# Cross-attention on one core: VectorE's sums interleaved, four products regrouped in PSUM, and the order of GpSimd's sums changed

## The chip, the cores and the metric

The kernel runs on one core of a Trainium2 chip. The metric is the device time of one execution in microseconds (us), and the median of the runs is compared. Engines are called as the profile calls them: PE (TensorE's matmuls), PEld (its weight loads), DVE (VectorE), ACT (ScalarE), POOL (GpSimd) and SP (SyncE, which here only issues DMAs). "Lnnn" is a line of the kernel file.

## The reference, cut to what matters

```python
q = jnp.einsum('bcn,dc->bnd', x1, Wq) + bq
k = jnp.einsum('bcn,dc->bdn', x2, Wk) + bk[:, None]
v = jnp.einsum('bcn,dc->bdn', x2, Wv) + bv[:, None]
attn = jax.nn.softmax(jnp.einsum('bnd,bdm->bnm', q, k), axis=2)
attn_out = jnp.einsum('bcm,bnm->bcn', v, attn)
return attn_out + x1
```

There are 8 batches; x1 and x2 have 512 channels and 1024 positions each, q and k have 64 channels. Everything is float32.

## The kernel before, in words

**The algebra.** The kernel never forms v. With e = exp(scores - maximum), transposed, it computes y = x2 · e (512 x 512 x 1024 after the halves are put side by side), scales y by one over the column sums of e, and then computes result = Wv · y + bv + x1. Both big products are done by a Strassen-Winograd scheme: the left and the right factor are cut into 2 x 2 quarters ("11", "12", "21", "22"), four sums of left quarters (S1 to S4) and four of right quarters (T1 to T4) are formed, and seven products take the place of eight. The table `MULT` says which left and right block each product takes and in which PSUM bank pair (a or c) it is accumulated. The products of y run in the order 1, 2, 6, 5, 7, 3, 4, those of the result in the order 1, 6, 2, 5, 7, 3, 4. One batch is one pass of `period`. I number batches from 0, as the code does (`s.b`); the batch after s is called n, the one after that nn.

**Plain and in blocks.** A plain product of y is 8 matmuls of 128 x 512 columns (`multiply`, L365); a plain product of the result is 4. The trace records each float32 matmul as two instructions, so a row with "x16" is a plain product of y and one with "x8" is a plain product of the result. A product "in blocks" is split by the same seven-product scheme once more: `inner_left` (L412, four DVE operations) and `inner_right` (L421, three) form its inner sums, and seven inner products (`inner_product`, L438) of two matmuls of 128 x 256 take the place of eight quarters: 14 matmuls of 128 x 256, each row "x4" being one inner product. Two ways exist to collect the inner products:

- `multiply_seeded` (L459): the chain of products 1, 6, 5 is accumulated in one buffer of the pool `ps_s`, product 7 in the other; ACT copies the chain at the right moments into two fresh banks of the pool `ps_a` (L479), where the other inner products are accumulated on it, and `complete` lets DVE add the copy of product 7, v, onto the second bank (L485). In y this is used for products 1, 2 and 7 from batch 1 on, and for product 3 everywhere.
- `multiply_onto` (L489): the inner products are accumulated on banks that hold an earlier sum already; the chain is copied to SBUF (d, L451), DVE adds v to d (L516), and d has to be added later by DVE to what stood in the bank. It is used for product 4 of y in every batch (`multiply_4`, which adds d to u6, L524) and for product 5 in batches 1 to 5 (`multiply_5`, L531, two additions). Product 5 of batches 6 and 7 and product 6 of every batch are plain, as are all products of the result.

**From y to the result.** After product 7, `evict_y("22")` reads bank c (L556); after product 3, `evict_t3` (L539) forms T3 from bank a and a copy u7 of bank c (`copy_7`, L534); after product 4, `evict_y("21")` reads bank c and u6. `scale_y` multiplies with the inverse sums (L547), `sum_y` forms the right sums T2, T1, T4 of the second scheme (L343). In the result, products 1, 6, 2 come first; `evict_o` (L567) adds the bias, GpSimd adds x1 by an accumulating DMA (L616), SP stores. Product 7 opens bank c, `evict_o("22")` reads that bank and u5 on DVE (L612), product 3 runs meanwhile in bank a, and product 4 is accumulated on bank c, so it has to wait until `evict_o("22")` has read it.

**What runs beside.** While batch s is in its products, the scores of batch n are computed (L228), copied out by ACT (L237), folded to a maximum over tiles by DVE (`fold`, L248; `fold_halves`, L252), reduced over partitions by GpSimd (`highest`, L258), lowered by that maximum on DVE (`lower`, L293) and raised by ACT (L297). The column sums of e for half 0 of batch n, in batches 1 to 6, are made off DVE: ACT copies tile 0 (`copy_first`, L625), and three accumulating DMAs of 512 KB, issued by GpSimd, add tiles 1, 2 and 3 (`add_tile`, L620). Each of them waits for the landing of the one before. `total` (L260) then folds the two halves on DVE (L252) and sums over partitions on GpSimd (L263). GpSimd also issues the additions of x2 quarters onto S1, S2, S3 (L159, L171) and of x1 onto the results.

**What sets the order.** The order of all work is written out by hand in `period` (`manual_schedule`), and each engine runs its instructions in the order in which they are issued there. PSUM: `ps_s` has two buffers, `ps_a` one bank each for a0, a1, c0, c1, so that a new use of bank a or c waits for the last reader of its old content. The end of `period` before, from product 4 of y on, reads in short: sums for product 4, scalings, T2, T1, product 4 (with `add_tile(2)` among its inner products), its eviction, T4, the maxima of (n, half 1), `highest`, `add_11(S3)`; products 1, 6 of the result, x1 onto u6; product 2, its eviction, `add_tile(3)`; product 5, the exponentials of (n, half 1), product 7, `evict_o("22")`, the inner sums of the next products 1 and 2, product 3, `evict_o("12")`, product 4, `total(n, 0)`, `evict_o("21")`.

Of the kernel before, what the change touches and what calls it, by code (L numbers as in the profile page):

```python
# [9 lines left out]
F32 = mybir.dt.float32  # L10
# [5 lines left out]
def kernel(  # L16
# [47 lines left out]
    nc = tc.nc  # L64
# [184 lines left out]

    def fold_halves(s, h, op):  # L250
        f = s.mx[h]
        nc.vector.tensor_tensor(f[:, 0, :], f[:, 0, :], f[:, 1, :], op)  # L252
# [41 lines left out]

    def exponential(s, h, i):
        e = s.e[h][:, :, i, :]
        nc.scalar.activation(e, e, AF.Exp)  # L297
# [39 lines left out]
    def sum_e(s, *ks, of=(0, 2)):  # L337
        for i in of:
            part = {n: v[:, i : i + 2, :] for n, v in s.t.items()}
            for k in ks:  # L340
                right_sums(part, k)

    def sum_y(s, k):  # L343
# [5 lines left out]
        else:  # L349
            nc.vector.tensor_tensor(y[k], y["22" if k == "T1" else "21"], y["T2"], ALU.subtract)  # L350

# [60 lines left out]
    def inner_left(s, i, x, tag):  # L412

        v = {f"{p + 1}{q + 1}": x[:, ts(q, MH // 2), ts(p, P)] for p in range(2) for q in range(2)}
        sums = sb.tile([P, 4, MH // 2, P], F32, tag=tag, name=f"aI{i}_{s.b}")
        for z, (k, x, y, op) in enumerate(LEFT):
            v[k] = sums[:, z]
            nc.vector.tensor_tensor(v[k], v[x], v[y], op)  # L418
        s.inner[i] = v

    def inner_right(s, i, x, *tags):  # L421

        v = {
            f"{q + 1}{r + 1}": x[:, ts(q, MH // 2), ts(r, H // 2)] for q in range(2) for r in range(2)
        }
        last = 4 // len(tags)
        shape = [P, last, MH // 2, H // 2]
# [5 lines left out]
        )  # L433
        nc.vector.tensor_tensor(t2, both[:, 0], v["22"], ALU.subtract)
        nc.vector.tensor_tensor(t4, v["21"], t2, ALU.add)
        s.inner[i, "t"] = v | {"T1": both[:, 0], "T3": both[:, 1], "T2": t2, "T4": t4}

    def inner_product(s, i, z, ps, opens, *copies):  # L438

        ka, kb, _, _ = MULT[z]  # L440
        for k in range(MH // 2):
# [5 lines left out]
                stop=z in (2, 3, 4) and k == MH // 2 - 1,  # L447
# [11 lines left out]
    def multiply_seeded(s, i, v_tag, hooks={}):  # L459

        bank = MULT[i][2]
        b0, b1 = (
            ps_a.tile([P, H], F32, tag=f"{bank}{j}", name=f"ps_y{bank}{j}_{s.b}_{i}") for j in range(2)
        )
        s.bank[bank, 0], s.bank[bank, 1] = b0, b1
        chain, third = inner_parts(s, i)
        v = sb.tile([P, 2, H], F32, tag=v_tag, name=f"v{i}_{s.b}")[:, 0, left]
        for z, ps, opens, out, of in (
            (1, chain, True, b0[:, left], chain),
            (7, third, True, v, third),  # L470
            (6, chain, False, b1[:, left], chain),
            (2, b0[:, left], False, None, None),
            (5, chain, False, b0[:, right], chain),
# [548 lines left out]
```

## Time and profile before

| what | value |
|---|---|
| time, median of 3 runs | 682.66 us (682.51 to 682.8) |
| span of the profiled execution | 680.8 us, 7209 instructions |
| outside the span, against the median | 1.86 us |
| PE busy | 672.1 us, 99% |
| DVE busy | 615.2 us, 90% |
| ACT busy | 336.9 us, 49% |
| POOL busy | 218.5 us, 32% |
| DMA | 131.09 MB, mean 193 GB/s |

The profiled execution's own time isn't given beside its span, so sums are made against the span, and the 1.86 us to the median of the runs are kept as they are. A row of a timeline has the start, the time from the first start to the last end of its group, the engine, the line, what is written and read, how many instructions the group holds, and in brackets the idle time before it and what ended that.

### The profile page before, as it was taken

What the parts mean: (1) busy time and instruction counts of PE and PEld (TensorE: products, weight loads), DVE (VectorE), ACT (ScalarE), POOL (GpSimd) and SP (SyncE); (2) the same over time, 40 slices, a digit from 0 to 9 for tenths busy, and PEclk for the clock granted to TensorE, in tenths of its full rate; (3) what the DMA queues carried; (4) which work ended last, traced back from release to release, by engine and by line L of the source; (5) the groups of instructions that cost most, each with busy time, mean ns of one, the idle gap of its engine ahead of it and who ended that gap; (6) DMA issues with size and microseconds to landing.
All of it is one profiled execution on the core that took longest, in us unless ns stands there. A gap on an engine that the chain in (4) does not pass through costs nothing.

```text
span 680.8 us, 7209 instructions
## 1 busy us (share of the span) xinstructions
PE 672.1 (99%) x2420; PEld 397.9 (58%) x2420; DVE 615.2 (90%) x763; ACT 336.9 (49%) x564; POOL 218.5 (32%) x182
## 2 busy tenths in 40 slices
PE   8999999999999999999999999999999999999997
PEld 5333554757547565566656576464854747556763
DVE  1999998899999999999999998999989979999884
ACT  2734266365554564544644637446475356553320
POOL 0124215251153502643125421344213451154100
PEclk9999999999999999999999999999999999999999
DMA  9656658967798759969499693996947985489503
GB/s 300 271 191 241 155 212 139 240 138 246 180 249 221 154 202 253 214 185 245 123 297 199 174 264 116 280 212 160 277 89 174 222 194 110 92 146 268 144 13 110
DMA packets 50772, 131.09 MB, mean 193 GB/s; under 512 B 5552, under 2 KB 7856, under 8 KB 50736
## 3 DMA queue, kind: packets, MB, share of 16 engines
q0 software_dynamic: 22464, 54.60, 44.7%
q1 hardware_dynamic: 27984, 75.64, 30.8%
q10 hardware_dynamic: 288, 0.39, 0.2%
q8 instruction: 19, 0.31, 0.2%
q14 instruction: 17, 0.14, 0.1%
HBM read 87.30 MB, written 16.81 MB: 153 GB/s over the span
## 4 chain that ended last, share of the span: by engine, by line
PE 84%; DVE 6%; DMA 5%; issue 2%; ACT 1%; SPq 1%; POOL 1%; DVEq 0%; POOLq 0%; ACTq 0%
PE ps_ya L380 11%; PE ps_oa L380 11%; PE ps_yc L442 8%; PE ps_oc L380 7%; PE ps_ya L442 6%; PE ps_s L228 5%; PE ps_o L400 4%; PE ps_o L380 4%; PE ps_k L181 3%; PE ps_q L181 3%; PE ps_i4chain L442 3%; PE ps_i3chain L442 3%; PE ps_i7chain L442 2%; PE ps_i1chain L442 2%; PE ps_i2chain L442 2%
## 5 line engine op out<-in xcount | busy, mean ns | idle before, releaser
L263 POOL PARTITION_ALL_REDUCE den<-sum x16 | 52.6, 3285 | 97.4 <-DVE few L271 60.3
L258 POOL PARTITION_ALL_REDUCE top<-max x16 | 37.6, 2352 | 126.3 <-DVE max L252 75.7
L380 PE MATMUL ps_ya<-eT,aS 128*128 128x512 f32 x176 | 77.5, 594 | 0.0
L293 DVE TENSOR_TENSOR e<-e,top 128x1024 f32<-128x1024 f32 x60 | 69.9, 1218 | 0.0
L620 POOL DMA_DIRECT2D sum<-e x21 | 32.1, 1530 | 108.7 <-ACT sum L625 42.0
L297 ACT ACTIVATE e<-e 128x1024 f32<-128x1024 f32 x60 | 61.8, 1058 | 4.7 <-DVE e L293 4.0
L380 PE MATMUL ps_oa<-yT,w_S 128*128 128x512 f32 x128 | 57.5, 592 | 0.0
L380 PE MATMUL ps_oc<-yT,w 128*128 128x512 f32 x128 | 57.4, 592 | 0.0
L380 PEld LDWEIGHTS ps_ya<-eT,aS 128*128 128x128 f32 x176 | 33.2, 190 | 40.1 <-issue 37.9
L237 ACT COPY e<-ps_s 128x1024 f32<-128x1024 f32 x46 | 45.6, 1032 | 9.0 <-PE ps_s L228 8.8
L228 PE MATMUL ps_s<-q,k 64*128 64x512 f32 x188 | 47.9, 608 | 0.9 <-ACT q L647 0.8
L380 PEld LDWEIGHTS ps_oa<-yT,w_S 128*128 128x128 f32 x128 | 24.3, 190 | 30.6 <-issue 30.6
L380 PEld LDWEIGHTS ps_oc<-yT,w 128*128 128x128 f32 x128 | 24.3, 190 | 30.6 <-issue 29.2
L248 DVE TENSOR_TENSOR max<-max,e 128x1024 f32<-128x1024 f32 x30 | 36.7, 1225 | 2.2
L391 ACT COPY uo<-ps_oa 128x512 f32<-128x512 f32 x32 | 18.7, 586 | 34.9 <-PE ps_oa L380 34.9
L391 ACT COPY uy<-ps_ya 128x512 f32<-128x512 f32 x24 | 13.9, 588 | 36.8 <-PE ps_ya L380 36.8
L228 PEld LDWEIGHTS ps_s<-q,k 64*128 64x128 f32 x188 | 17.1, 186 | 24.5 <-issue 18.0
L479 ACT COPY ps_ya<-ps_i1chain 128x256 f32<-128x256 f32 x28 | 10.0, 357 | 42.2 <-PE ps_i1chain L442 38.7
L547 DVE TENSOR_TENSOR y<-y,den 128x1024 f32<-128x1024 f32 x24 | 29.3, 1221 | 0.3
L418 DVE TENSOR_TENSOR aI<-a 128x256 f32<-128x256 f32 x58 | 29.4, 547 | 0.0
L380 PE MATMUL ps_oa<-y,w_S 128*128 128x512 f32 (+1 forms) x68 | 28.8, 567 | 0.0
L400 PE MATMUL ps_o<-y,w 128*128 128x512 f32 x64 | 28.8, 592 | 0.0
(202 smaller groups left out, 1539.0 us busy)
## 6 DMA issues: line engine op xcount, KB each, us to landing
x_in_x_dram<-in_x_dram SPq DMA_DIRECT2D x60, 512.0 KB, 7.6
a<-in_x2T_dram SPq DMA_DIRECT2D x32, 512.0 KB, 10.1
sum<-e POOLq DMA_DIRECT2D x21, 512.0 KB, 10.1
aS<-in_x2T_dram POOLq DMA_DIRECT2D x14, 512.0 KB, 8.9
uo<-in_x_dram POOLq DMA_DIRECT2D x14, 512.0 KB, 9.9
r<-in_x_dram POOLq DMA_DIRECT2D x14, 512.0 KB, 12.2
out_dram<-r SPq DMA_DIRECT2D x14, 512.0 KB, 6.5
eT<-eT POOLq DMA_DIRECT2D x14, 512.0 KB, 10.1
```

The source lines that it names most:

```text
L181: nc.tensor.matmul(ps[r, :], w_sb[:, c, :], s.x[:, c, ts(h, H)], start=(c == 0), stop=(c == CT - 1),)
L228: nc.tensor.matmul(ps[g], s.k[r, ts(i, P)], s.q[r, ts(h, H)], start=True, stop=True)
L237: nc.scalar.copy(e[:, :, i, :], whole)
L248: nc.vector.tensor_tensor(f, e[:, :, 0, :] if i == 1 else f, e[:, :, i, :], op)
L258: nc.gpsimd.partition_all_reduce(s.top[h], s.mx[h][:, 0, :], P, ReduceOp.max)
L263: nc.gpsimd.partition_all_reduce(s.den[h], s.mx[h][:, 0, :], P, ReduceOp.add)
L293: nc.vector.tensor_tensor(e, e, top, ALU.subtract)
L297: nc.scalar.activation(e, e, AF.Exp)
L380: nc.tensor.matmul(ps[:, n], left[ka][:, k, ts(j, P)], right[kb][:, k, n], start=opens and k == 0, stop=i in (2, 3, 4) and k == n_k - 1, s ...
L391: nc.scalar.copy(s.tmp[i][:, j, :], ps)
L400: nc.tensor.matmul(ps, w["11"][:, k, ts(j, P)], s.y["11"][:, k, :], start=k == 0, stop=False, skip_group_check=True)
L442: nc.tensor.matmul(ps, s.inner[i][ka][:, k, :], s.inner[i, "t"][kb][:, k, :], start=opens and k == 0, stop=z in (2, 3, 4) and k == MH // 2 ...
```

## The change

Five things are changed; everything else stays.

1. **Weaving.** `inner_left`, `inner_right`, the folds and the lowerings become generators, and `weave` issues several independent streams in turn, one operation of each, so that a DVE operation less often directly follows the one whose result it reads. `sum_e` issues its operations in another order from batch 1 on.
2. **Fresh banks in y.** From batch 1 on, products 5, 3 and 4 of y are done by `multiply_seeded`, in banks a, c and c (a for product 4 of the last batch). The additions of d vanish; in their place `join_67` adds u7 to u6 once, y22 is read from bank a and u6, T3 from bank c and u7, y21 from bank c (a in the last batch) and the joined u6. Product 5 is now in blocks in batches 6 and 7, too. In batch 0 the old forms stay.
3. **Product 7 of the result in blocks**, in batches 1 to 6 (`multiply_57`): seven matmuls of 128 x 256, issued in turns with those of the plain products 5 and 3. Its left sums are formed once (`left_values`), its right sums "o7" from yT3 by three DVE operations in each batch, woven with T4; `complete_7` is one more DVE addition.
4. **Order on DVE and GpSimd** in batches 1 to 5 (`five`): the folds of the maxima of (n, half 1) and `highest` stand ahead of product 4 of y; `add_tile(3)` and `add_11(S3)` stand directly behind the eviction of y21, ahead of its scaling; `total(n, 0)` stands ahead of `complete_7` and `evict_o("22")` instead of behind product 4 of the result.
5. **Last batch:** T3 of e is made by ACT and accumulating DMAs instead of DVE, and `total(s, 1)`, `invert`, `spread` and `shares` move.

The diff, cut to its core:

```diff
+    def weave(*streams):
+
+        streams = list(streams)
+        while streams:
+            for stream in list(streams):
+                if next(stream, "end") == "end":
+                    streams.remove(stream)
...
+    def multiply_57(s):
+
+        s.inner["o7"] = inner_w["o7"]
+        bank = [ps_a.tile([P, H], F32, tag=f"c{j}", name=f"ps_oc{j}_{s.b}_7") for j in range(2)]
+        s.bank["c", 0], s.bank["c", 1] = b0, b1 = bank
+        chain, third = inner_parts(s, "o7")
+        v = sb.tile([P, 2, H], F32, tag="aI3", name=f"vo7_{s.b}")[:, 0, left]
+        s.tmp[5] = sb.tile([P, 2, H], F32, tag="u5", name=f"uo5_{s.b}")
...
+        plain(5, 0, 0, 1)
+        inner_product(s, "o7", 1, chain, True, b0[:, left])
+        inner_product(s, "o7", 7, third, True, v)
+        plain(5, 1, 0)
+        inner_product(s, "o7", 6, chain, False, b1[:, left])
+        inner_product(s, "o7", 2, b0[:, left], False)
+        plain(5, 1, 1)
+        inner_product(s, "o7", 5, chain, False, b0[:, right])
+        inner_product(s, "o7", 4, b1[:, left], False)
+        nc.scalar.copy(b1[:, right], chain)
+        plain(3, 0, 0)
+        inner_product(s, "o7", 3, b0[:, right], False)
+        plain(3, 0, 1)
+        plain(3, 1, 0, 1)
...
-    def multiply_5(s, hooks):
-
-        d, complete = multiply_onto(s, 5, "u5", "r", hooks)
-        complete()
-        for j in range(2):
-            nc.vector.tensor_tensor(d[:, j, :], s.bank["a", j], d[:, j, :], ALU.add)
-        s.tmp[5] = d
+    def join_67(s):
+        nc.vector.tensor_tensor(s.tmp[6], s.tmp[6], s.tmp[7], ALU.add)
...
             if n:
-                lower(n, 0, 0)
+                weave(right_stream(s, 3, s.t["22"], "eT1"), lowers(n, 0, 0, 1))
+            else:
+                inner_right(s, 3, s.t["22"], "eT1")
             complete_7 = multiply_seeded(s, 7, "y12")
             complete_7()
-            evict_y(s, "22")
...
+            copy_7(s, 0)
+            if n:
+                lower(n, 0, 1)
+            complete_3 = multiply_seeded(s, 3, "r", hooks, "c")
...
+            join_67(s)
+            evict_y(s, "22")
...
+                for i in range(2, MH):
+                    lower(n, 0, i)
             complete_3()
             evict_t3(s)
...
-            inner_left(s, 4, s.a["22"], "a12")
-            inner_right(s, 4, s.t["T4"], "eT2")
+            weave(left_stream(s, 4, s.a["22"], "a12"), right_stream(s, 4, s.t["T4"], "eT2"))
         if late:
             scale_y(s, "11", "T3", "22")
         sum_y(s, "T2")
-        sum_y(s, "T1")
+        if s.b == 0:
+            sum_y(s, "T1")
+        if five:
+            weave(folds(n, 1, "max", ALU.max))
+            highest(n, 1)
...
-        multiply_4(s, hooks)
+        if s.b == 0:
+            multiply_4(s, hooks)
+        else:
+            complete_4 = multiply_seeded(s, 4, "r", hooks, "c" if n else "a")
+            complete_4()
...
         evict_y(s, "21")
+        if n is None:
+            sum_y(s, "T1")
+        if five:
+            add_tile(n, 0, 3)
+            add_11(n, "S3")
         scale_y(s, "21")
-        sum_y(s, "T4")
         if late and n:
-            for i in range(1, MH):
-                fold(n, 1, i, "max", ALU.max)
+            sum_y(s, "T1")
+        if five:
+            weave(iter_t4(s), right_stream(s, "o7", s.y["T3"], "eT1"))
...
+        blocks = s.b >= FIRST_O and n is not None
+        if blocks:
+            complete_7 = multiply_57(s)
+        else:
+            second(5)
...
-        second(7)
+        if blocks:
+            if five:
+                total(n, 0)
+            complete_7()
+        else:
+            second(7)
...
             evict_o(s, "12")
             second(4)
-            total(n, 0)
+            if not five:
+                total(n, 0)
             evict_o(s, "21")
```

More of the change, by code (lines that the diff above doesn't have):

```diff
@@ L248, in fold, with folds @@
         nc.vector.tensor_tensor(f, e[:, :, 0, :] if i == 1 else f, e[:, :, i, :], op)
+    def folds(s, h, kind, op):
+        for i in range(1, MH):
+            fold(s, h, i, kind, op)
+            yield
     def fold_halves(s, h, op):
@@ L553, in evict_y @@
         bank, add = RESULT[k]
+        if s.b and k == "22" or s.b == B - 1 and k == "21":
+            bank, add = "a", 6
         s.y[k] = y = sb.tile([P, 2, H], F32, tag=f"y{k}", name=f"y{k}_{s.b}")
```

191 lines of the change are left out of this document (124 added, 67 removed).

## The prediction

> **What bounds the kernel now.** I read the page first (busy shares and the chain that ended last), then a table of windows from one product 1 of y to the next, then PE's timeline for its stalls, then DVE's and POOL's around product 4 of y.
>
> ```profile
> span 680.8 us, 7209 instructions
> ...
> PE 672.1 (99%) x2420; PEld 397.9 (58%) x2420; DVE 615.2 (90%) x763; ACT 336.9 (49%) x564; POOL 218.5 (32%) x182
> ```
> ```profile
> PE 84%; DVE 6%; DMA 5%; issue 2%; ACT 1%; SPq 1%; POOL 1%; DVEq 0%; POOLq 0%; ACTq 0%
> ```
> ```profile
> 120.46:204.21 83.75, 82.86 (x306) 50.71 (x305) 77.71 (x99) 44.21 (x74) 28.93 (x24) 1.00 0.87 210
> ...
> 286.25:368.24 81.99, 81.99 (x306) 50.52 (x304) 77.88 (x99) 43.72 (x74) 28.96 (x24) 1.00 0.83 208
> ...
> 532.41:608.83 76.42, 76.13 (x261) 46.05 (x260) 70.70 (x88) 41.49 (x68) 28.71 (x24) 1.00 0.69 147
> 608.83:680.80 71.97, 68.16 (x233) 43.87 (x231) 56.00 (x74) 18.71 (x41) 11.83 (x11) 1.00 0.50 138
> ```
>
> The last four rows are batches 1, 3, 6 and 7 (length, then busy time of PE, PEld, DVE, ACT, POOL, then the granted clock). In batch 3 PE is busy for all of its 81.99 us at clock 1.00, so time falls only where PE gets less work or a stall of PE goes. DVE has 77.88 us of work in the same window: 4.1 us of slack, so a DVE operation that moves can come late for PE.
>
> **PE's work.** Product 6 of y (plain), product 7 (in blocks), products of the result:
>
> ```profile
> 298.33 7.03 PE L380 MATMUL ps_ya<-eT,aS 128*128 128x512 f32 x16
> 305.29 1.13 PE L228 MATMUL ps_s<-q,k 64*128 64x512 f32 x4
> ...
> 318.66 1.03 PE L442 MATMUL ps_i7chain<-e,a 128*128 128x256 f32 x4
> ...
> 324.70 1.03 PE L442 MATMUL ps_i3chain<-e,aS 128*128 128x256 f32 x4
> ```
> ```profile
> 344.21 3.60 PE L400 MATMUL ps_o<-y,w 128*128 128x512 f32 x8
> ...
> 364.81 3.60 PE L380 MATMUL ps_oc<-yT,w 128*128 128x512 f32 x8
> 368.24 1.03 PE L442 MATMUL ps_i1chain<-e,a 128*128 128x256 f32 x4
> ```
>
> From start to start, a plain result product takes 368.24-364.81 = 3.43 (six before it: 20.60/6 = 3.43). A plain product of y is two of these, 6.87 (the rows show 6.96, with the change of shape behind it). In blocks it takes 324.70-318.66 = 6.04, so an inner product takes 0.863 and one matmul of 128 x 256 0.4315.
>
> - Product 7 of the result in blocks: 7 x 0.4315 = 3.02 for 3.43, so -0.41 in each of batches 1 to 6: **-2.5**. Its matmuls stand in turns with plain ones of 128 x 512; where the shape changes at 305.29 the step is 0.09 long, and I put such switches into the 0.2 below. The cover it needs is ACT's (seeds) and DVE's (three right sums, woven with T4, some 8 us ahead of need).
> - Product 5 of y in blocks in batches 6 and 7: 2 x (6.87-6.04): **-1.7**.
> - Products 3 and 4 in fresh banks, and 5 in batches 1 to 5: the same matmuls, 0. What they change is who waits.
>
> **Stalls that go or come.**
>
> ```profile
> 165.05 1.99 PE L228 MATMUL ps_s<-q,k 64*128 64x512 f32 x8
> 167.94 1.29 PE L228 MATMUL ps_sa<-q,k 64*128 64x512 f32 x3 [0.89 <-DVE yT L542]
> ```
> ```profile
> 577.88 1.13 PE L442 MATMUL ps_i4chain<-eT,a 128*128 128x256 f32 x4
> 579.29 1.13 PE L442 MATMUL ps_i4third<-eI4eT,aI 128*128 128x256 f32 x4 [0.29 <-ACT e L237]
> ```
>
> In batch 1 the scores' tile in bank a waits until T3 has been read from bank a: 0.89 idle, and 0.17 more because a row's end overlaps the next start (3.60 against 3.43). After the change product 3 is in bank c, and bank a was last read for y22, before product 3 ended, so the stall goes: **-1.1**. What is late next there is product 4's bank c, which T3 frees about 5 us before product 4's first seed.
>
> In batch 6 no k projection stands between the scores and product 4, and its second inner product comes 1.41 after the first, where a step is 0.86. It needs DVE's first left and right sum for product 4. Those were begun right behind T3; now `join_67`, y22 and two lowerings stand ahead of T3. Working forward as below, I get these sums at about 1.2 behind need where it was 0.55-0.7: **+0.5**. Between 0 (ACT is named in the row, not DVE) and 1.0.
>
> Other new inner sums (products 1, 2, 5, 7, 3) come 2 to 5 us ahead of need by the same count, so weaving them is worth nothing on PE by itself. Product 1 of the result needs DVE no more than before. Head and tail are left as they are; the last batch loses a 1.2 us DVE sum to ACT and DMAs that have 6 us to spare. Shape switches and product 7 of batch 6, borderline: **+0.2**, between -0.3 and +0.9.
>
> **The wait that decides: product 4 of the result.** Before, `total(n, 0)` stood behind product 4 on PE and nobody on PE waited for it:
>
> ```profile
> 369.37 0.69 DVE L252 TENSOR_TENSOR sum<-sum 128x512 f32<-128x512 f32 x1 [0.22 <-DMA sum<-e]
> ```
>
> Now this fold stands on DVE ahead of `complete_7` and `evict_o("22")`, and product 4 needs bank c from that eviction. The chain is: maxima, all-reduce, `add_tile(2)`, its landing, `add_tile(3)`, its landing, fold, `complete_7`, eviction, PE. Behind the waiting fold are queued on DVE also the inner sums of the next products 1 and 2, needed some 3 us later than product 4; behind `add_tile(3)` on GpSimd are queued S3's addition and x1 onto u6 and the first result, whose stores on SP come 1 to 3 us later, with nothing of PE's due within 10 us.
>
> First, when does GpSimd get to `add_tile(2)`? It now stands behind `highest`, so behind the folds of the maxima on DVE. DVE's prices and the anchor:
>
> ```profile
> 349.14 1.22 DVE L248 TENSOR_TENSOR max<-e 128x1024 f32<-128x1024 f32 x1
> 350.40 2.48 DVE L248 TENSOR_TENSOR max<-max,e 128x1024 f32<-128x1024 f32 x2
> 352.91 0.69 DVE L252 TENSOR_TENSOR max<-max 128x512 f32<-128x512 f32 x1
> 353.52 1.60 DVE L418 TENSOR_TENSOR aI<-a 128x256 f32<-128x256 f32 x2
> 355.15 0.88 DVE L418 TENSOR_TENSOR aI<-a,aI 128x256 f32<-128x256 f32 x2
> 355.95 4.62 DVE L293 TENSOR_TENSOR e<-e,top 128x1024 f32<-128x1024 f32 x4
> ```
> ```profile
> 332.31 0.75 DVE L418 TENSOR_TENSOR aI<-a 128x256 f32<-128x256 f32 x2
> ...
> 336.48 1.22 DVE L547 TENSOR_TENSOR y<-y,den 128x1024 f32<-128x1024 f32 x1
> ```
> ```profile
> 326.63 0.37 ACT L479 COPY v<-ps_i3third 128x256 f32<-128x256 f32 x1 [0.51 <-PE ps_i3third L442]
> ```
>
> An independent 128x1024 operation comes (4.62-1.22)/3 = 1.13 after the one before, one that reads its predecessor's result 350.40-349.14 = 1.26; a 128x512 one 353.52-352.91 = 0.61. So weaving saves 0.12 for each broken dependence. The sums for product 4 took 336.48-332.31 = 4.17; woven, four dependences go: 3.69.
>
> The Trainium skill, in "VectorE: DVE Perf Modes", section "The DRAIN you can't avoid", says that a semaphore between chained VectorE operations costs nothing extra (eight copies took the same time with a semaphore after each as with one after the last). By that, weaving would shorten nothing; the 1.26 against 1.13 here speaks against it.
>
> Anchor, on the clock of before in batch 3: ACT's copy of product 3's v ends at 327.00, its copy of u7 about 0.7 later, so `join_67` starts at 327.75. Then DVE has: join 1.26, y22 1.21, two lowerings 2.27, `complete_3` 0.61, T3 1.21, sums for product 4 3.69, three scalings 3.40, T2 1.13, three folds 3.77, halves 0.69: 19.24, ending at 347.0. So GpSimd's maximum starts at 347.1:
>
> ```profile
> 337.07 1.23 POOL L620 DMA_DIRECT2D sum<-e  x1 [11.79 <-ACT sum L625]
> ...
> 345.11 1.19 POOL L620 DMA_DIRECT2D sum<-e  x1 [5.87 <-ACT e L297]
> 353.71 1.88 POOL L258 PARTITION_ALL_REDUCE top<-max  x1 [7.41 <-DVE max L252]
> ...
> 357.46 2.56 POOL L620 DMA_DIRECT2D sum<-e  x1
> ```
> ```profile
> 431.18 1.19 POOL L620 DMA_DIRECT2D sum<-e  x1 [8.76 <-ACT ps_oa L404]
> ...
> 442.42 1.18 POOL L620 DMA_DIRECT2D sum<-e  x1 [1.42 <-DMA sum<-e]
> ```
> ```profile
> 582.08 1.20 POOL L620 DMA_DIRECT2D sum<-e  x1 [13.81 <-ACT d L451]
> 587.87 1.19 POOL L620 DMA_DIRECT2D sum<-e  x1 [4.59 <-ACT ps_oa L404]
> ```
> ```profile
> 344.40 1.41 SPq L144 DMA_DIRECT2D a<-in_x2T_dram  x3
> ```
> ```profile
> DMA to landing us min/median/max: 5.0/10.1/13.1
> ```
>
> 347.1 + 1.88 lets `add_tile(2)` start at about 348.9, 3.8 later than before (345.11). From one such issue to the next that waits for its landing it takes 5.79 with nothing beside (batch 6: 582.08 to 587.87), 8.04 in batch 3 (337.07 to 345.11), 11.24 in batch 4 (431.18 to 442.42). I take **8.04**, the middle: the three a loads (344.40) are under way for 4.5 us when it starts, where before it went out together with them. So `add_tile(3)` starts at 356.9 (before 357.46). It now goes ahead of S3's and x1's additions instead of behind them (landing before 369.35 by the fold's start), so I give it 5.79: landing 362.7. Second, the deadline: products 1, 6, 2 and then 5, 7, 3 of the result: 344.21 + 3 x 3.43 + 9.88 = 364.4, less fold 0.07 + 0.61, `complete_7` 0.61, eviction 0.75, 0.06 = 2.1: 362.3. So PE waits about 0.4 in each of batches 1 to 4: **+1.5**. Batch 5 has no batch after the next whose x would be loaded (the row of batch 6 shows what that does to DMA's share: 0.69 for 0.83), so I count its sums at the 5.79 of batch 6 and nothing there.
>
> The sum: -2.5 - 1.7 - 1.1 + 0.5 + 0.2 + 1.5 = -3.1 on the profiled 680.8, that is 677.7; with the 1.86 that separate span and median, **679.6**. About 0.2% (1.4 us) is what a measurement of this kernel tells from no change.
>
> **Rivals.**
>
> - *Sums land late (slower).* If `add_tile(2)` takes 11.24 as in batch 4, landing is 365.9, 3.6 late in each of four batches: +14.2 in place of +1.5, 692.3. If 2 takes 10.1 (the median) and 0.5 to issue, and 3 takes 5.4 (between 5.0 and 5.79), it is 364.9, 2.6 late: 688.5. All else saves 4.6, so it decides from 1.15 us of wait per batch, landing at 363.45. For: the median landing is 10.1, and DMA is busy 0.83 of these windows. Against: the a loads have a head start now, and tile 3 is alone. 0.25, at about 688.5.
> - *No wait.* If either DMA gains 0.4 us the wait is gone: -4.6, 678.1; without batch 6's borderlines 677.5. For: the lone rows, 5.79 and 5.0. 0.18. The Trainium skill ("DMA: Bandwidth & Descriptors", section "Anatomy of one DMA — SWDGE (gpsimd) path") has 2.0 us + bytes/436e3, an estimate of 3.2 us for 512 KB, which would give this case; no row here is under 5.0.
> - *Nothing visible.* Three waits like batch 6's (0.5 to 1.0) come in the batches where I count 2 us of margin, because DVE's fronts slip by the stretch seen at 353.52 (1.60 for two 128x256 beside the all-reduce, where 332.31 shows 0.75); such a 0.85 at five places eats 3 to 4 us: 682 to 683. 0.10.
> - *Weaving saves nothing.* Then the maxima end 0.5 later, and each of four waits is 0.5 longer: 681.6. 0.02.
>
> **How the numbers follow.** My forecast holds 0.45, with its own range 678.3 to 681.2. Faster: 0.45 + 0.18 = 0.63; within 0.2%: 0.10 + 0.02 = 0.12; slower 0.25. The range reaches from the no-wait case with its borderlines (676.8) to the middle of the late sums (689.0), which leaves out the rest of that rival and little below.
>
> **What would show it.** In the changed profile: from product 1 to product 1 in batch 3, 81.6 plus the wait; product 7's seven inner rows at 0.43; no idle time at the scores' tile in bank a of batch 1; product 4 of the result with idle time in brackets, its releaser DVE's eviction, and DVE's fold of the sum waiting for the DMA just ahead. `add_tile(3)` issued about 12.7 after product 1 of the result started, its fold at 18.5. If the fold comes before 18.1, the wait is none; after 19.2 I am wrong about the sign.

## The result, and the profile after

| kernel | median, us | runs | lowest to highest | ratio to before | 95% interval |
|---|---|---|---|---|---|
| before | 682.59 | 4 | 682.17 to 682.8 | | |
| after | 692.03 | 4 | 689.01 to 693.26 | 1.0139 | 1.0118 to 1.0160 |

The change makes the kernel 1.4% slower. The forecast was 679.6 with a range up to 689.0. Two things are visible at once: the time lies where the first rival (sums land late, 688.5 to 692.3) put it, and the runs spread over 4 us where those of before spread over 0.6. The profiled execution is the fastest of the four: span 687.0, 2.0 under its time of 689.01.

First the page of after: its busy shares and the chain that ended last.

```profile
span 687.0 us, 7460 instructions
...
PE 669.5 (97%) x2480; PEld 408.6 (59%) x2480; DVE 605.0 (88%) x795; ACT 350.2 (51%) x602; POOL 215.3 (31%) x184
...
PE 38%; DMA 10%; issue 6%; DVE 5%; ACT 2%; POOL 1%; DVEq 0%; POOLq 0%; ACTq 0%
```

PE's work fell, as forecast (672.1 to 669.5). The chain that ended last can't be set share against share: after's is followed back only as far as 264.09 us, so its shares add up to 62% of the span and before's to 100%. Of what is followed, PE was 84 parts in 100 and is 38 in 62, DMA was 5 in 100 and is 10 in 62: waits for DMA have entered the chain. The views that say where come next: the windows from one product 1 of y to the next, for batches 1 to 7 (length, busy time of PE, PEld, DVE, ACT, POOL, granted clock, DMA share, GB/s).

```profile
119.13:201.71 82.58, 81.85 (x311) 51.45 (x310) 72.88 (x97) 45.74 (x79) 29.07 (x25) 1.00 0.85 210
201.71:285.38 83.67, 81.85 (x311) 51.45 (x310) 74.66 (x101) 45.65 (x79) 28.03 (x26) 1.00 0.83 205
285.38:367.86 82.48, 81.85 (x311) 51.44 (x310) 74.66 (x101) 45.66 (x79) 28.02 (x26) 1.00 0.83 207
367.86:452.34 84.48, 81.84 (x311) 51.45 (x310) 74.65 (x101) 45.65 (x79) 28.10 (x26) 1.00 0.83 203
452.34:533.92 81.58, 81.58 (x311) 51.54 (x310) 76.22 (x104) 45.66 (x79) 29.09 (x27) 1.00 0.81 189
533.92:609.75 75.83, 75.04 (x279) 49.17 (x278) 73.20 (x98) 43.35 (x76) 24.95 (x23) 1.00 0.68 144
609.75:687.00 77.25, 69.38 (x245) 47.02 (x243) 58.09 (x82) 21.33 (x46) 15.47 (x14) 0.98 0.55 145
```

Batch 5 is the forecast's batch: 81.58, all of it PE, 0.41 less than 81.99. Batches 1 to 4 are 1.00, 2.09, 0.90 and 2.90 longer than that. Batch 7 has become 5.28 longer (71.97 to 77.25), and its clock reads 0.98. Span against span: start of batch 1 -1.33 (it lies between 119.13 and 120.76 in the profiles of this study, 119.75 in one of them with before's code up to there, so I read nothing from it), batches 1 to 6 -1.17, +1.63, +0.49, +2.30, -0.41, -0.59, batch 7 +5.28: +6.2.

The waits of batches 2 and 4 on PE's timeline, then DVE's timeline ahead of the one in batch 4:

```profile
281.84 3.70 PE L394 MATMUL ps_oc<-yT,w 128*128 128x512 f32 x8 [1.82 <-DVE uo L702]
```
```profile
448.81 3.70 PE L394 MATMUL ps_oc<-yT,w 128*128 128x512 f32 x8 [2.64 <-DVE uo L702]
```
```profile
446.80 0.69 DVE L258 TENSOR_TENSOR sum<-sum 128x512 f32<-128x512 f32 x1 [5.34 <-DMA sum<-e]
447.41 0.69 DVE L541 TENSOR_TENSOR ps_oc<-ps_oc,vo 128x512 f32<-128x512 f32 x1
448.01 1.40 DVE L702 SCALAR_TENSOR_TENSOR uo<-ps_oc,bv_sb,uo 128x512 f32<-128x512 f32 x2
```

This is the chain that the prediction drew: DVE stands 5.34 us at the fold until the third sum has landed, then come `complete_7`, the eviction, and only then product 4 of the result. And the sums on POOL in batches 3 and 4:

```profile
347.76 1.25 POOL L710 DMA_DIRECT2D sum<-e  x1
356.79 1.19 POOL L710 DMA_DIRECT2D sum<-e  x1 [7.78 <-ACT vo L483]
```
```profile
431.34 1.22 POOL L710 DMA_DIRECT2D sum<-e  x1 [0.97 <-issue]
441.25 1.18 POOL L710 DMA_DIRECT2D sum<-e  x1 [8.69 <-DMA sum<-e]
```

From the second issue to the third it is 9.03 and 9.91, where the forecast took 8.04. Batch 5, which has no wait, shows what differs; below its two rows are SP's loads in batch 3 (four of x, then the three a loads) and in batch 5 (the three a loads alone):

```profile
514.73 1.25 POOL L710 DMA_DIRECT2D sum<-e  x1
520.34 1.19 POOL L710 DMA_DIRECT2D sum<-e  x1 [4.36 <-ACT r L697]
```
```profile
337.30 3.45 SPq L137 DMA_DIRECT2D x_in_x_dram<-in_x_dram  x4
343.53 1.41 SPq L144 DMA_DIRECT2D a<-in_x2T_dram  x3
...
510.50 1.28 SPq L144 DMA_DIRECT2D a<-in_x2T_dram  x3
```

In batch 5 the second sum goes out 4.2 us behind the three a loads, as in batch 3, and takes 5.61 to the next issue. There the a loads land 3.2 to 5.5 us after their issue; in batches 1 to 4, where the four loads of x go out some 6 us ahead of them, they take 7.3 to 12.7.

Batch 7, PE:

```profile
634.75 1.03 PE L474 MATMUL ps_i7chain<-e,a 128*128 128x256 f32 x4
639.33 2.04 PE L474 MATMUL ps_i7third<-eI7yT,aI 128*128 128x256 f32 x4 [3.55 <-DVE eI7yT L456]
641.17 1.67 PE L474 MATMUL ps_i7chain<-eI7yT,aI 128*128 128x256 f32 x4
642.67 1.03 PE L474 MATMUL ps_yc<-e,a 128*128 128x256 f32 x4
```
```profile
637.96 1.23 DVE L456 TENSOR_TENSOR eI7yT<-e 128x1024 f32<-128x1024 f32 x1 [3.69 <-DMA e<-e]
```

Product 7 waits for its right sum, and that for the DMA that forms T3. And the wait costs more than its 3.55: the next two inner products take 639.33 to 642.67, 3.34 instead of 1.73. The windows on either side of that place give the granted clock:

```profile
639.33:642.67 3.34, 3.34 (x8) 2.66 (x9) 3.31 (x10) 0.37 (x1) 0.43 (x1) 0.53 1.03 204
642.67:646.12 3.45, 3.45 (x17) 3.04 (x16) 2.70 (x4) 1.07 (x3) 1.24 (x3) 1.00 0.11 20
```

0.53 of full speed just after the wait, 1.00 from 642.67 on.

### The profile page after: what moved, and what is told of

Read it like the earlier page. It is cut to its first block, busy times and chain, and to the rows that moved or that the text cites. A ratio compares the mean times of both kernels' runs of the same rounds, so it can differ in the third digit from the quotient of the medians.

```text
span 687.0 us, 7460 instructions
## 1 busy us (share of the span) xinstructions
PE 669.5 (97%) x2480; PEld 408.6 (59%) x2480; DVE 605.0 (88%) x795; ACT 350.2 (51%) x602; POOL 215.3 (31%) x184
## 4 chain that ended last, share of the span: by engine, by line
PE 38%; DMA 10%; issue 6%; DVE 5%; ACT 2%; POOL 1%; DVEq 0%; POOLq 0%; ACTq 0%
DMA sum<-e 7%; PE ps_yc L474 5%; PE ps_ya L394 4%; PE ps_oc L394 3%; PE ps_ya L474 3%; PE ps_oa L394 3%; PE ps_s L228 2%; DMA e<-e 2%; PE ps_i1chain L474 2%; PE ps_i2chain L474 2%; PE ps_o L394 1%; PE ps_i7chain L474 1%; DMA row<-few 1%; PE ps_i3chain L474 1%; PE ps_o L414 1%
## 5 line engine op out<-in xcount | busy, mean ns | idle before, releaser
L394 PE MATMUL ps_ya<-eT,aS 128*128 128x512 f32 x144 | 63.5, 594 | 0.0
L394 PEld LDWEIGHTS ps_ya<-eT,aS 128*128 128x128 f32 x144 | 27.1, 190 | 32.2 <-issue 29.0
L394 PE MATMUL ps_oc<-yT,w 128*128 128x512 f32 x80 | 36.2, 597 | 5.8 <-DVE uo L702 5.8
L394 PE MATMUL ps_oa<-yT,w_S 128*128 128x512 f32 x80 | 36.1, 594 | 0.5 <-ACT ps_oa L418 0.5
L394 PEld LDWEIGHTS ps_oc<-yT,w 128*128 128x128 f32 x80 | 14.9, 190 | 26.4 <-issue 16.4
L706 POOL DMA_DIRECT2D r<-in_x_dram x14 | 29.1, 2078 | 1.6 <-ACT r L697 1.6
L258 DVE TENSOR_TENSOR sum<-sum 128x512 f32<-128x512 f32 x16 | 11.0, 689 | 20.7 <-DMA sum<-e 20.7
L284 POOL DMA_DIRECT2D den<-row x16 | 8.9, 559 | 64.5 <-DMA row<-few 64.5
L414 PE MATMUL ps_o<-y,w 128*128 128x512 f32 x64 | 28.8, 592 | 0.0
L394 PE MATMUL ps_o<-y,w 128*128 128x512 f32 x64 | 28.8, 592 | 0.0
L394 PEld LDWEIGHTS ps_oa<-yT,w_S 128*128 128x128 f32 x80 | 15.1, 190 | 20.0 <-issue 18.4
```

Source lines behind the costliest of these rows:

```text
L394: nc.tensor.matmul(ps[:, n], left[ka][:, k, ts(j, P)], right[kb][:, k, n], start=opens and k == 0, stop=i in (2, 3, 4) and k == n_k - 1, s ...
L414: nc.tensor.matmul(ps, w["11"][:, k, ts(j, P)], s.y["11"][:, k, :], start=k == 0, stop=False, skip_group_check=True)
L706: nc.gpsimd.dma_start(o, block(s, k, x1), accum_op=ALU.add)
```

## The experiments

My theory after this: two places make the whole loss, the early `total` in batches 1 to 5 and T3 by DMA in the last batch, and the rest gains what was forecast. Its rival: the added seeds on ACT and the interleaved order cost by themselves, and the waits only show it. The kernel before was run again beside each group of experiments: its median was 682.59 beside after, 681.97 beside 1 to 4, 681.88 beside 5 to 8, 682.26 beside 9 to 12. The ratios are against these, so a difference of two medians from different groups can be off by up to 0.7 us.

**1. `total` back behind product 4 of the result** (after, batches 1 to 5).

```diff
-            if five:
-                total(n, 0)
             complete_7()
...
             second(4)
-            if not five:
-                total(n, 0)
+            total(n, 0)
```

> The changed kernel, but the total of the next half 0 stands behind product 4 of the result again in batches 1 to 5, as before the change. Theory (the fold's wait for the third sum's landing holds bank c and so product 4): the idle time before product 4 of the result goes from 0.9, 2.0, 0.8 and 2.8 us in batches 1 to 4 to none, the span falls from 687.0 to about 680.1, the time to about 682.1 (still with the last batch's stall), and the runs spread by under 1 us instead of 4. Rival (the added load of ACT's seeds and of the earlier sums is what costs, the wait only shows it): the same 5 to 7 us turn up before other products, and the time stays above 687.

Measured: 683.51 (681.64 to 684.57, 11 runs), ratio to before 1.0023 (1.0014 to 1.0032). So 8.5 us go (7.9 by the ratios), more than the 6.9 of the profiled run, which was after's fastest and had its highest mean clock. Batch 3 of it and batch 7:

```profile
282.60:364.18 81.58, 81.58 (x312) 51.51 (x310) 75.49 (x101) 45.65 (x79) 27.94 (x26) 1.00 0.86 212
...
603.17:680.70 77.53, 69.42 (x245) 47.08 (x243) 58.09 (x82) 21.33 (x46) 15.47 (x14) 0.98 0.55 144
```

Batches 1 to 5 are all 81.58: no wait is left and none has taken its place. The rival falls for these batches. That the runs would lie within 1 us was wrong; they still spread over 2.9, in steps with the mean granted clock of the run: 681.64 at 1.000, 682.59 to 683.95 at 0.997, 684.02 to 684.57 at 0.995.

**2. T3 of the last batch on VectorE again** (after, otherwise).

```diff
-            sum_t3(s, 0)
-            sum_t3(s, 2)
+            if n:
+                sum_t3(s, 0)
+                sum_t3(s, 2)
...
             evict_y(s, "11")
+            if n is None:
+                sum_e(s, "T3")
             sum_t4(s)
```

> The changed kernel, but T3 of e in the last batch is formed by VectorE again. Theory (the two accumulating DMAs of T3, 9.2 and 10.7 us to landing, hold product 7 of y by 3.6 us, and PE then runs at half clock for 3.3 us): the last batch takes about 71.2 us instead of 77.25, the time falls by 6, to about 686 (683 to 687.5, since the waits of the other batches vary). Rival (VectorE is the limit of the last batch, the DMAs only relieve it): VectorE's two operations push its other sums back, another wait of 2 us or more takes the place, and the time falls by less than 3.5.

Measured: 690.55 (689.61 to 691.73, 4 runs), 1.0119 (1.0103 to 1.0135): about 1.5 less than after, where the theory had 6. Its batch 7 takes 76.16 (613.54 to 689.7): PE stands 2.28 us at the same place, now for DVE, and is slow behind it, too (granted clock 0.53 from 643.0 to 646.5). The theory is wrong by three quarters; the rival holds, with another wait of over 2 us in the place and less than 3.5 gained.

**3. Both** edits together.

> Both at once: total behind product 4 of the result, and T3 of the last batch on VectorE. Theory (these two places are the whole loss, and the rest of the change gains what the forecast counted): batches 1 to 5 take 81.58 each, the span is about 674.3 and the time 676.2 (675.5 to 677.5), 0.9% under the kernel before. Rival (the two are relieved, but fresh banks and weaving cost elsewhere): 679 or more.

Measured: 681.1 (680.13 to 682.41, 11 runs), 0.9990 (0.9981 to 0.9999): 2.4 under experiment 1, but 4.9 over the theory. Batches 1 to 5 are 81.58; batch 7 is what remains:

```profile
604.31:678.80 74.49, 67.91 (x245) 45.83 (x243) 60.18 (x84) 19.43 (x44) 13.81 (x12) 1.00 0.51 136
```
```profile
632.65 1.10 PE L474 MATMUL ps_i7third<-eI7yT,aI 128*128 128x256 f32 x4 [2.32 <-DVE eI7yT L456]
```

74.49, where before had 71.97 with a plain product 5. DVE isn't waiting for a DMA there: it comes late by its own work, to which the inner sums of product 5 were added.

**4. Experiment 3 with product 7 of the result plain.**

```diff
-    FIRST_O = 1
+    FIRST_O = 9
```

> As the kernel with both places undone, and product 7 of the result plain in all batches. Theory (product 7 in blocks saves 0.41 us in each of six batches and waits for nothing): 2.5 us more than with it, about 678.7. Rival (its seeds and right sums cost as much on ACT and DVE as PE gains): within 0.7 us of the kernel with both places undone.

Measured: 683.59 (682.63 to 685.52, 9 runs), 1.0028 (1.0018 to 1.0037): 2.5 more than experiment 3. Its batches 1 to 5 are 81.99 each, so product 7 in blocks is worth 0.41 in each of these batches, to the hundredth, and 0.42 in batch 6 (76.25 against 75.83). The rows carry this; the medians, whose runs spread over 2 to 3 us, agree.

**5. Experiment 3 with product 5 of the last batch plain**, in a fresh bank a, without `sums_5`.

```diff
-                weave(*sums_5)
...
+            if n:
+                complete_5 = multiply_seeded(
...
+            else:
+                for j in range(2):
+                    s.bank["a", j] = ps = ps_a.tile([P, H], F32, tag=f"a{j}", name=f"ps_ya{j}_{s.b}_5")
+                    for k in range(MH):
+                        nc.tensor.matmul(
...
+                            s.a["S1"][:, k, ts(j, P)],
+                            s.t["T1"][:, k, :],
...
```

> As the kernel with both places undone, and product 5 of y in the last batch plain (in a fresh bank), so without its seven inner sums on VectorE. Theory (VectorE is the limit of the last batch: product 7 there waits 2.3 us for sums that stand behind 3.75 us of product 5's): PE's 0.83 is lost, but the idle time before product 7's second inner product goes, the last batch takes about 72.7 us instead of 74.5, the time falls by 1.8. Rival (product 7's sums wait for something else of the new order in the last batch, T3 or S4): the idle time stays over 1.5 us and the time rises by 0.8.

Measured: 678.63 (677.8 to 679.12, 5 runs), 0.9950 (0.9937 to 0.9962). PE has 0.83 more work and the time falls by 2.5; batch 7 is 72.73 and no idle time stands before product 7. So product 5 in blocks, worth 0.83 on PE, cost DVE 3.75 that the last batch didn't have: from the start of the batch to the half-sum that follows (L258) DVE takes 20.68 with its sums and 16.93 without.

**6. Experiment 3 without weaving:** `weave` runs each stream to its end before the next.

> As the kernel with both places undone, and without weaving: each stream is issued whole before the next. Theory (a broken dependence saves 0.12 us of VectorE, which has 2 to 5 us of margin in batches 1 to 5 and none in the last two): batches 1 to 5 stay at 81.58, batches 6 and 7 together lose 0.3 to 1.5. Rival (weaving saves nothing, a wait between chained operations is free): no batch changes by 0.2 and the time is within 0.3. Second rival (weaving delays the first sum that PE needs): 0.5 or more faster.

Measured: 683.67 (682.2 to 686.03, 11 runs), 1.0029 (1.0018 to 1.0039): 2.6 more. Batches 1 to 5 stay at 81.58; batch 6 goes from 75.83 to 78.15 and batch 7 from 74.49 to 75.23. On PE's and DVE's timelines of batch 6:

```profile
576.47 1.10 PE L472 MATMUL ps_i4third<-eI4eT,aI 128*128 128x256 f32 x4 [1.90 <-DVE eI4eT L454]
```
```profile
573.52 0.75 DVE L439 TENSOR_TENSOR aI<-a 128x256 f32<-128x256 f32 x2
574.30 0.88 DVE L439 TENSOR_TENSOR aI<-a,aI 128x256 f32<-128x256 f32 x2
575.10 1.22 DVE L454 TENSOR_TENSOR eI4eT<-eT 128x1024 f32<-128x1024 f32 x1
```

The first right sum, which PE needs second, starts 47.68 after the batch began; in experiment 3 it starts at 573.65, 45.17 after. Half of these 2.51 isn't the 0.12 per dependence but the order: without weaving that sum stands behind all four left sums, 1.58 after the first of them instead of 0.33. The other 1.26 DVE is late already when the left sums begin. Weaving brings the first operation of each stream forward. It pays in the last two batches only, where PE stands next to DVE; the 3.05 that they lose together is above my range of 0.3 to 1.5.

**7. After, with the second sum issued ahead of the maximum's all-reduce.**

```diff
             weave(folds(n, 1, "max", ALU.max))
-            highest(n, 1)
...
             complete_4()
+        if five:
+            highest(n, 1)
```

> The changed kernel, but the maximum's all-reduce of the next half 1 stands behind the issue of the second sum on GpSimd, not ahead of it. Theory (the landing of the third sum decides; the second is held on GpSimd behind the all-reduce by 3.7 us, and its own landing takes 8.5 to 9.7 beside three loads): the second sum is issued some 3.5 earlier but takes about 10.3, so the third lands 1.5 to 2.5 earlier; the waits of batches 1 to 3 (0.9, 2.0, 0.8) go or fall under 0.5, that of batch 4, where the first sum landed late, stays at 2.8; the time falls by 3 to 4. Rival (what is late is VectorE, not the sum): the waits stay as they are.

Measured: 687.58 (686.03 to 688.02, 4 runs), 1.0078 (1.0064 to 1.0092), 4.4 less. POOL in batch 3:

```profile
342.12 1.19 POOL L710 DMA_DIRECT2D sum<-e  x1 [5.85 <-ACT ps_yc L561]
344.47 1.78 POOL L264 PARTITION_ALL_REDUCE top<-max  x1 [1.15 <-DVE max L258]
352.90 1.21 POOL L710 DMA_DIRECT2D sum<-e  x1 [6.65 <-ACT r L697]
```

Its product 1 of the result starts at 341.23, so the second sum goes out 0.9 after it instead of 4.4 (347.76 against 343.34), takes 10.78 to the next issue, and the third goes out 11.7 after instead of 13.5. The waits of batches 1 to 3 are gone; that of batch 4 stays (batch of 84.43). The waits moved as the theory had it, and the time fell by a little more than the 3 to 4 expected.

**8. After, with SP's loads of x2 quarters moved behind product 6 of the result in the program.**

```diff
-        if n:
+        if n and not five:
             load_a(n, "12")
-        if nn:
+        if nn and not five:
             load_a(nn, "21", "22")
...
             add_x1(s, "21")
+        if five:
+            load_a(n, "12")
+        if nn and five:
+            load_a(nn, "21", "22")
```

> The changed kernel, but in batches 1 to 5 the three loads of x2 quarters that SP issues beside the second sum come behind product 6 of the result, some 7 us later. Theory (the second sum takes 8.5 to 9.7 us because it shares the DMA engines with these three loads): it lands in 5 to 6, the third sum is issued 3 us earlier, the waits before product 4 go in all batches unless the third sum now takes over 8 beside the loads, and the time falls by 6 to 8. Rival (the landing depends on the sum's own accumulation or on GpSimd's queue): the second sum still takes over 8, and the waits change by less than 1 us each.

Measured: 692.0 (689.23 to 693.86, 4 runs), 1.0139 (1.0114 to 1.0164): no difference, because nothing moved. The loads go out 0.2 us after product 1 of the result in both kernels: SP has nothing to do in between, and a later place in a queue without other work is no later time. It tells nothing of the theory.

**9. The same loads on ACT's queue,** behind the copies of product 6.

```diff
         second(6)
+        if five:
+            load_a(n, "12", engine=nc.scalar)
+            if nn:
+                load_a(nn, "21", "22", engine=nc.scalar)
```

> The changed kernel, but the three loads of x2 quarters are issued by ACT's queue behind the copies of product 6 of the result in batches 1 to 5, so some 7 us later; issued by SP, moving them in the program moved nothing, since SP sent them as soon as product 4 had freed their tile. Theory (the second sum takes 8.5 to 9.7 us since it shares the DMA engines with them): it lands in 5 to 6.5, the third is issued 2 to 3.5 us earlier; if it still lands in 5.5 to 7 the waits before product 4 of the result go in batches 1 to 3 and fall under 1.5 in batch 4, and the time falls by 3 to 8. Rival (the sums are slow by themselves): the second still takes over 8, the waits stay.

Measured: 685.06 (684.63 to 686.3, 4 runs), 1.0044 (1.0030 to 1.0058), 7 less than after. POOL in batch 3:

```profile
345.71 1.25 POOL L710 DMA_DIRECT2D sum<-e  x1
351.56 1.19 POOL L710 DMA_DIRECT2D sum<-e  x1 [4.61 <-ACT r L697]
```

From second to third 5.85 instead of 9.03, with the loads out of the way; batches 1, 2, 3 and 5 are 81.58, batch 4 is 81.77. So the three loads beside it made the second sum late. They don't by themselves: in batch 5 of after the same three loads are beside it and it takes 5.61. What batches 1 to 4 have besides are the four loads of x that SP sends some 6 us ahead; behind those alone, as here, it takes 5.85. It is late where all seven are under way. No run takes only the loads of x away, so this last point rests on batch 5.

**10. The kernel before, with `total` ahead of `evict_o("22")` alone** (batches 1 to 5, product 7 of the result plain).

```diff
         second(7)
+        if late and n and nn:
+            total(n, 0)
...
             second(4)
-            total(n, 0)
+            if not (late and nn):
+                total(n, 0)
```

> The kernel before, with one thing changed: the total of the next half 0 ahead of the eviction of the result's 22 quarter in batches 1 to 5, the sums begun as late as ever. Theory (product 4 of the result waits for the landing, the fold and the eviction): the third sum lands at 25.1 us after product 1 of the result started, product 4 is due at 20.6 and would start at about 27.2, so 6.5 us idle in each of five batches, and after idle times of that length PE runs at half clock for some 3.4 us, 1.7 more each: about 40 us, 722. Rival (the fold gets ahead without harm, since the sums land earlier when PE doesn't press): under 10 us.

Measured once: 724.04, span 722.3. Batch 3 on PE and DVE:

```profile
386.41 6.56 PE L380 MATMUL ps_oc<-yT,w 128*128 128x512 f32 x8 [5.82 <-DVE uo L612]
```
```profile
385.00 0.69 DVE L252 TENSOR_TENSOR sum<-sum 128x512 f32<-128x512 f32 x1 [8.80 <-DMA sum<-e]
```

About 6 idle, and product 4 takes 6.40 to the next start instead of 3.43: the granted clock is 0.55 from 386.41 to 392.81. That the time is so near the 722 expected is partly luck: the idle times are 5.69 to 6.28, not 6.5, and the slow clock costs 1.6 to 3.0 each, not 1.7. The order of this one fold is worth some 42 us when the sums aren't begun earlier; with the earlier sums of the change it costs 8.5, not 0.

**11. Experiment 5, with T3 of the last batch by ACT and DMA as in the change:** the edit of experiment 2 taken back.

> As the kernel with the last batch's product 5 plain, but T3 of e there by ACT and two accumulating DMAs as in the change. Theory (the DMAs' landing is late by itself, VectorE's load or not): the second lands about 28 us after the batch's product 1, product 7's second inner product wants its sum at 26.7 and gets it at 29.4, so 2.5 to 3.5 us of idle time and up to 1.7 of half clock, 681 to 683. Rival (the DMAs were late only because VectorE's folds, woven with product 7's left sums, held ACT back): no wait, 678.6 as without.

Measured: 682.22 (681.23 to 683.75, 10 runs), 1.0002 (0.9992 to 1.0011): 3.6 more than experiment 5. So T3 by DMA is late without DVE's extra load as well, by less than the theory had (another 0.66 is idle before product 5, for ACT's copies):

```profile
633.25 1.13 PE L474 MATMUL ps_i7third<-eI7yT,aI 128*128 128x256 f32 x4 [1.75 <-DVE eI7yT L456]
```

**12. Experiment 5 with two more moves on DVE:** batch 6's lowering of tile 3 behind product 4's sums, the last batch's completion and eviction of y21 ahead of T2.

```diff
-                for i in range(2, MH):
+                for i in range(2, MH if nn else 3):
                     lower(n, 0, i)
...
+            if nn is None:
+                lower(n, 0, 3)
...
         evict_y(s, "21")
         if n is None:
+            sum_y(s, "T2")
+            scale_y(s, "22")
             sum_y(s, "T1")
```

> As the kernel with the last batch's product 5 plain, and two more moves on VectorE: in batch 6 the lowering of tile 3 comes behind the sums for product 4 instead of ahead of T3; in the last batch the completion and eviction of y21 come ahead of T2 and of the scaling of y22. Theory (the 0.6 us before product 4's sums in batch 6 is VectorE's one lowering too much, the 0.67 before product 6 of the result in the last batch is bank a, which y21's eviction holds): both idle times go, the span falls from 676.5 by 1.2, the time to about 677.4. Rival (another wait ends as late in each place): under 0.3.

Measured: 677.35 (677.01 to 677.98, 5 runs), 0.9929 (0.9917 to 0.9942), the fastest kernel of this study, 0.7% under before. PE of its batch 6 and its last batch:

```profile
574.58 1.13 PE L474 MATMUL ps_i4third<-eI4eT,aI 128*128 128x256 f32 x4 [0.29 <-ACT e L237]
```
```profile
647.65 3.60 PE L414 MATMUL ps_o<-y,w 128*128 128x512 f32 x8
651.09 3.60 PE L394 MATMUL ps_oa<-yT,w_S 128*128 128x512 f32 x8
```

The second of the last two stood like this in experiment 3, and 4.11 after the first, both there and in experiment 5:

```profile
654.17 3.70 PE L394 MATMUL ps_oa<-yT,w_S 128*128 128x512 f32 x8 [0.51 <-ACT ps_oa L418]
```

The last batch's 0.67 has gone (651.09 - 647.65 = 3.44), so bank a, which y21's eviction held, was its cause. The move in batch 6 changed nothing: the wait there is ACT's copy of a score, as its row says and as it stood in before's row; I had put it down to DVE. That the time is the 677.4 expected, with one of the two moves doing nothing, is luck: the profiled span fell by 0.9, not 1.2.

## Why the prediction was wrong, point by point

Two steps make the miss of 12.4 us: the wait for the third sum, counted at 1.5 and measured at 8.5, and the last batch, where product 5 was counted as a gain of 0.83 and T3 as nothing, and which lost 4.9 by the two. That is 7.0 and 5.7; the rest of the terms nearly cancel.

- **Product 7 of the result in blocks, -2.5:** right; 2.5 by experiment 4 against 3.
- **Product 5 in batches 6 and 7, -1.7:** wrong. The failing step is "Other new inner sums (products 1, 2, 5, 7, 3) come 2 to 5 us ahead of need by the same count": it was counted in batch 3 and carried to the last batch ("Head and tail are left as they are"), where the margin isn't there. In batch 6 the 0.83 is nearly eaten by a new wait of 0.66 for ACT's copy of a score, since product 5 in blocks needs a `ps_s` buffer and a plain one doesn't (the row below). In batch 7 it cost 2.5 net (experiment 5); in before's last batch the first right sum of product 7 is ready at 634.60 and wanted at 635.52, 0.9 ahead, and the 3.75 us of product 5's sums now stand in front of it.

```profile
557.17 1.13 PE L474 MATMUL ps_i5chain<-eT,aS 128*128 128x256 f32 x4 [0.50 <-ACT e L237]
```

- **The stall in batch 1, -1.1:** right in kind, too small: from the scores to k it was 5.39 in before (165.05 to 170.44 on PE's timeline) and 3.63 in other batches, so 1.76. I counted the 1.06 of the first row. Bank a has two halves, and a wait for the second would account for the rest; no row names it.
- **Batch 6's product 4, +0.5:** 0.0. The row named ACT, and ACT it was.
- **The last batch's T3, "ACT and DMAs that have 6 us to spare":** the worst step, given in half a sentence without a row. The scaling on ACT waits for the folds that read the same tile; the two DMAs go out 14.5 and 17.4 us after the batch began and land 9.2 and 10.7 later (624.22 to 633.43, 627.16 to 637.83), the second of them after the 635.61 at which product 7 wants the sum made from it. 3.6 by experiment 11 against 5. Nor is it a "1.2 us DVE sum" that went: in before's last batch it is two operations of 2.77 together.

```profile
626.57 2.77 DVE L306 TENSOR_TENSOR e<-e 128x1024 f32<-128x1024 f32 x2
```

- **Fresh bank a for product 4 of the last batch, counted at 0:** it put 0.67 ahead of product 6 of the result (experiment 12).
- **The wait for the third sum, +1.5:** the mechanism is exactly the one drawn, and the deadline holds; the size is 6.9 in the profiled run and 8.5 between the medians. The failing step is "I take 8.04, the middle: the three a loads (344.40) are under way for 4.5 us when it starts", which took the head start as a relief. The second issue came 4.4 after product 1 of the result in batches 1 to 3, 0.3 earlier than worked out (5.5 in batch 4, where the first sum landed late), and took 9.0 to 10.3 to the next: after 4.4 us the loads were still under way, since they stand behind four loads of x (5.85 with the three moved away, experiment 9; 5.61 with the three but no x ahead of them, batch 5). For batch 5 the prediction itself took 5.79 and no wait, and was right. The third sum's landing, taken as 5.79, was 5.5.
- **Weaving:** no gain in batches 1 to 5, as said; 2.3 in batch 6 and 0.7 in batch 7, which I had not seen.
- **The chances:** the slower rival had 0.25 and the price of 688.5 to 692.3, which is where the time is, though its mechanism makes only 8.5 of the 13.4 us lost; that the time lies at its price is luck. A deadline met to within 0.4 by a DMA whose own rows ran from 5.79 to 11.24 was no likeliest case; with 9.6, the middle between 8.04 and 11.24, each of the four waits would have been 1.6 longer and the forecast 686.0.

The waits of after at product 4 and the last batch's T3 and product 5 are 8.5 (after to experiment 1), 2.4 (1 to 3) and 2.5 (3 to 5), together 13.4 of 692.03 (by the ratios 7.9, 2.3 and 2.7, together 12.9). What is left of the change, 678.63, is 0.5% faster than before (experiment 5): 3.25 under the 681.88 measured beside it, where I forecast 3.1 for the whole. That the two agree is luck, since the forecast has a wait of 1.5 and a gain of 0.83 in batch 7 that this kernel doesn't have. How much of the head's -1.33 is chance stays open.

## What to carry to other kernels

When an operation that waits for a DMA is moved ahead of work that another engine needs, the DMA's landing joins the critical path with its whole spread, so price it by the slowest landing of the rows beside the same traffic, not by the middle. A transfer's head start over another is worth something only if it isn't itself queued behind others: look at when it lands, not at when it was issued. Count margins for the last pass of a pipelined loop by itself: there, the work that fills the gaps in the other passes is missing, and an operation that is free everywhere else can cost most of its length. A later place in the program moves a transfer only if its queue has something to wait for.

## What the runs showed of the hardware

**An idle PE comes back at half clock, from 2.3 us of idle time on, but not always.** After 3.55 us idle the granted clock was 0.53 for 3.34 us, and it was low after all ten waits of 3.5 us or more from batch 1 on. After shorter ones it was a matter of chance: of the nine waits between 2.28 and 2.67 us in the profiles, from batch 1 on, three were followed by a low clock (2.28 and 2.29 in experiment 2, 2.67 in experiment 8) and six were not. 2.64 idle in after's batch 4 left the clock at 1.00 (product 4's row: 3.70 long), and 2.29 idle in experiment 2's batch 2 halved it:

```profile
283.93 5.40 PE L394 MATMUL ps_oc<-yT,w 128*128 128x512 f32 x8 [2.29 <-DVE uo L702]
```
```profile
284.00:287.50 3.50, 3.50 (x5) 1.58 (x6) 3.50 (x6) 0.08 (x1) 3.20 (x4) 0.56 1.12 205
```

The two shown cost 1.6 to 1.7 us more. Others cost up to 3.0: in experiment 9 the clock is 0.50 for all of 634.25 to 639.50, in experiment 10 it is 0.55 from 386.41 to 392.81. The Trainium skill ("TensorE: Matmul & The Clock Gate", section "Part 1: The HAM clock gate (the "warmup" mystery)") describes a monitor with a free-running window of about 3.4 us, after an idle one of which the clock is halved until a busy one has passed. The lengths of the slow stretches, from about one such window to less than two, and the chance agree with that; that 2.28 us of idle time were enough does not, if a whole window has to be idle. The slow clock seems to make most of after's spread: its four runs took 689.01 at a mean clock of 0.997, 691.17 at 0.995, 692.89 and 693.26 at 0.993, and 0.004 of 690 us are 2.8 of the 4.25, an estimate.

**A sum of 512 KB by an accumulating DMA lands in 5.5 us** where its path is clear (the third sum, in batches 1 to 5 of after), in 5.1 with three loads of the same size issued 4.2 us ahead of it (the second sum in batch 5), and in 8.5 to 9.7 where these three stand behind four others (batches 1 to 4).
